# Group means of the normalisation in two PSUM banks, and a fold of the softmax sums moved behind a semaphore word, in a two-layer attention kernel

## The chip, the cores and the metric

The kernel runs on one core of one Trainium2 chip. The metric is the device time of one execution in microseconds (us), as the median over several executions. Five engines matter: TensorE (PE in the profile; PEld is its loading of weights), VectorE (DVE), ScalarE (ACT), GpSimd (POOL) and SyncE (SP, here only a queue that issues DMAs). GpSimd also issues DMAs, namely those that add to their target.

## The reference

The input x has 16 images of 256 channels by 32 by 32 positions, fp32. Two layers follow each other; each normalises in 16 groups along the last axis, runs attention with 4 heads of 64 channels over 1024 positions with a position term, and adds the result to x.

```python
def _gn(v, G=16, eps=1e-5):
    g = v.reshape(B_, H_, W_, G, C_ // G)
    m = jnp.mean(g, axis=(1, 2, 4), keepdims=True)
    s = jnp.var(g, axis=(1, 2, 4), keepdims=True)
    return ((g - m) / jnp.sqrt(s + eps)).reshape(v.shape)

q, k, v = proj(Wq, bq), proj(Wk, bk), proj(Wv, bv)      # 1x1 convolutions
sim  = jnp.einsum('bhdi,bhdj->bhij', q, k)
qpos = jnp.einsum('hdi,bhdj->bhij', (rel_h + rel_w).reshape(heads, d, n), q)
attn = jax.nn.softmax(sim + qpos, axis=-1)
x    = x + jnp.einsum('bhdn,bhmn->bhdm', v, attn)       # twice, for two layers
```

The part that the change touches is small arithmetic: the mean and the variance of each group, a sum over 128 partitions of a table of 16 columns, and the sums of the softmax.

## The kernel before

**Units and blocks.** A unit `u` is one image in one layer; there are 32, in the order of the list `units`. Each unit has four blocks `b` = 0 to 3: two pairs of heads (`pr`) times two halves of the query columns (`half` = `b` % 2). So there are 128 blocks, numbered `n`, and `block(n)` (from line 647) writes the instructions of all engines for one of them. The kernel schedules by hand: each engine executes its instructions in the order of this program text, and an instruction that waits holds up all that stand behind it on its engine.

**What a block does.** Eight score tiles `ps` of 128 by 1024 are made: VectorE first writes the position term into PSUM (`seed`, line 346), TensorE adds q k on top (`scores`, line 382), ScalarE takes the exponential into `p` (line 391), VectorE adds the `p` tiles up for the softmax sums (`add_up`, lines 400 and 402). Then TensorE forms v^T p in a PSUM tile `po` (`attend`, line 416). The seeds and first scores of the next block (`after`) are already made in the tail of the current one. Between them stand pieces of the next pair of heads or the next unit: projections q, k (line 265), values (line 295), position terms (line 323).

**Stretches and words.** All these products use TensorE as four tiles of 64 by 64, so that matmuls of the lower and the upper 64 rows run side by side. [...] So a product over 128 rows comes in two stretches: in the first the lower rows write bank 0 and the upper ones bank 1, in the second the other way round. Between the two stands a "word" (`stretches`, line 166): a one-element memset by GpSimd that waits for the last matmul of the first stretch, and for which the first matmul of the second stretch waits. In the text of a block, `values_of_p(0)` is the first stretch of v^T p, `values_of_p.word()` its word, `values_of_p(1)` its second stretch.

**The group means.** Unit `u + 2` is normalised while unit `u` is worked on. ScalarE sums the columns of each group (`norm_sums`, `norm_squares`, line 190). At the end of block 1 (`norm_mean`) and of block 3 (`norm_var`) TensorE sums over the partitions with a constant matrix `W.avg` (`mean_of_rows`, line 210) into `pm`, 16 columns of one bank, zeroed by VectorE (line 202). This too is a product in two stretches: `mean(0)` with the lower rows right after `values_of_p(0)`, then the scores of the next block's first tile, then `mean(1)` with the upper rows, then `values_of_p(1)`. `mean(1)` calls its own word on GpSimd. ScalarE takes the result out (`mean_out`): as the negated mean `neg` (line 220), or as `var` with epsilon added (line 232), after which GpSimd computes `rstd` by a power (line 234) and `nshift` (line 236). The next block, block 0 of the next unit, starts to apply them (`norm_apply`, line 245). Thirty units do this in the loop, that is 60 means.

**The softmax sums.** GpSimd's DMAs add, "fold", the accumulated tile of a block: the eighth `p` onto `acc` (`add_last`, line 433), the upper half of `acc` onto the lower (`fold`, line 438), parts onto a `stack` of the four sums of a pair of heads (SP in `stack_up`, line 452, and GpSimd in `fold_again`, line 457), and the stack onto itself with 64, 32, 16, 8 and 4 rows (`fold_stack`, line 462). Each fold of the stack needs the one before to have landed, and its issue on GpSimd waits for that. `spread_sums` (SP, line 470) distributes the result, `reciprocals` (lines 512 to 519) inverts it in the next block, and `finish` (lines 527 and 534) normalises the output and adds it to x.

**The order in the tail of a block with half = 1**, on GpSimd: the fold with 32 rows, `fold` of the previous block, the folds with 16 (`R // 2`) and 8 rows (`R // 4`), the word of v^T p, the word of the mean, the fold with 4 rows (`R // 8`), `fold_again`, in block 3 the power, and then, of the next block, `add_last` and the word `first.word()` of its first piece. On VectorE: the seed of the next block's first tile, the memset of `pm`, `add_up(5)`, the two instructions of `finish`, three seeds of the next block.

## Time and profile before

| | |
|---|---|
| runs | 2557.47 us median of 3 (2554.66 to 2560.26) |
| the profiled execution | 2574.55 us, span in the profile 2572.8 us |
| clock granted to TensorE | 0.997 of full speed, mean over the span |
| TensorE busy | 98% of the span |
| VectorE, ScalarE, GpSimd busy | 88%, 76%, 33% |
| matmuls of the means, line 210 | 30.3 us busy in all (15.3 and 15.0) |
| memsets of the words, line 166 | 190 |
| power on GpSimd, line 234 | 30, median 3.88 us each |

The profiled execution is 17 us longer than the median of the runs. Times of single instructions below are from the profiled execution. "Idle before" of a group is the time for which its engine stood still just ahead of it, and the profile names what ended that wait. A weight load (PEld) can wait without TensorE's stream standing still, since loads run ahead of matmuls.

### The profile page before, as it was taken

How to read it: one execution, taken by the hardware profiler on the slowest of the kernel's cores; microseconds unless marked ns; L12 is line 12 of the kernel's file. 1: busy time of each engine (PE TensorE's matmuls, PEld its weight loads, DVE VectorE, ACT ScalarE, POOL GpSimd, SP SyncE). 2: the span in 40 equal slices, each digit the busy share in tenths (PEclk: the TensorE clock that was granted, in tenths of full speed). 3: DMA queues.
4: the chain of work that ended last, by engine and by line, in shares of the span. 5: the costliest groups of instructions: out<-in, count | busy, mean ns of one | idle time of the engine just before them, and what ended most of it. 6: DMA issues, size and time to landing. Idle time of an engine off the chain costs nothing. (4 is left out here: it accounts for less than half of the span.)

```text
span 2572.8 us, 86074 instructions
## 1 busy us (share of the span) xinstructions
PE 2524.8 (98%) x37474; PEld 1739.3 (68%) x37474; DVE 2258.1 (88%) x2076; ACT 1956.9 (76%) x3934; POOL 837.4 (33%) x1254
## 2 busy tenths in 40 slices
PE   8999999999999999999999999999999999999997
PEld 4667776666777656666767777677776776666774
DVE  6888998888888889899888898898898998988997
ACT  6778777787777887777877777877778777787753
POOL 1232333323333233333233333333332333323320
PEclk9999999999999999999999999999999999999999
DMA  3344444444444444444444444444445444444441
GB/s 89 72 80 82 78 86 76 90 96 90 84 99 99 82 82 92 89 88 87 93 85 86 98 87 78 92 98 90 91 85 106 79 78 90 77 77 78 88 84 57
DMA packets 119539, 221.06 MB, mean 86 GB/s; under 512 B 53737, under 2 KB 55273, under 8 KB 119153
## 3 DMA queue, kind: packets, MB, share of 16 engines
q0 software_dynamic: 53568, 129.58, 30.3%
q1 hardware_dynamic: 65584, 85.90, 12.1%
q8 instruction: 295, 4.83, 0.8%
q14 instruction: 92, 0.75, 0.1%
HBM read 51.78 MB, written 17.30 MB: 27 GB/s over the span
## 5 line engine op out<-in xcount | busy, mean ns | idle before, releaser
L346 DVE TENSOR_TENSOR ps<-abt 128x1024 f32<-128x1024 f32 x1018 | 1225.7, 1227 | 279.3 <-ACT p L391 160.4
L391 ACT ACTIVATE p<-ps,shift 128x1024 f32<-128x1024 f32 x1024 | 1092.2, 1114 | 326.9 <-PE ps L382 237.5
L382 PE MATMUL ps<-q,k 64*64 64x512 f32 x8192 | 1016.3, 590 | 0.8 <-DVE ps L346 0.8
L416 PE MATMUL po<-p,v 64*64 64x256 f32 x16384 | 950.9, 378 | 0.0
L416 PEld LDWEIGHTS po<-p,v 64*64 64x64 f32 x16384 | 826.2, 133 | 140.9 <-issue 45.6
L402 DVE TENSOR_TENSOR acc<-acc,p 128x1024 f32<-128x1024 f32 x644 | 783.7, 1217 | 5.3 <-ACT p L391 0.5
L382 PEld LDWEIGHTS ps<-q,k 64*64 64x64 f32 x8192 | 409.5, 133 | 300.7 <-issue 186.7
L462 POOL DMA_DIRECT2D stack<-stack x310 | 254.1, 820 | 544.2 <-DMA stack<-stack 281.2
L166 POOL MEMSET token<- 1x1 f32 x380 | 47.9, 126 | 763.1 <-PE po L416 477.4
L295 PE MATMUL pv<-Wv,xn 64*64 64x256 f32 x4096 | 251.9, 376 | 2.4 <-POOL token L166 2.1
L265 PE MATMUL pq<-xn,Wq 64*64 64x512 f32 x2048 | 252.0, 593 | 0.3 <-DVE xn L906 0.3
L265 PE MATMUL pk<-xn,Wk 64*64 64x512 f32 x2048 | 250.4, 590 | 0.9 <-POOL token L166 0.9
L295 PEld LDWEIGHTS pv<-Wv,xn 64*64 64x64 f32 x4096 | 203.4, 133 | 56.7 <-issue 39.2
L457 POOL DMA_DIRECT2D stack<-acc x248 | 223.6, 1088 | 43.0 <-issue 29.7
L245 ACT ACTIVATE xn<-x,nshift,rstd 128x128 f32<-128x128 f32 x496 | 211.1, 500 | 16.3 <-POOL nshift L236 16.3
L190 ACT ACTIVATE junk<-x,neg 128x128 f32<-128x128 f32 x498 | 195.0, 400 | 0.0
L265 PEld LDWEIGHTS pq<-xn,Wq 64*64 64x64 f32 x2048 | 108.4, 134 | 112.3 <-issue 107.0
L438 POOL DMA_DIRECT2D acc<-acc x124 | 102.4, 826 | 251.6 <-DMA acc<-p 239.3
L477 ACT COPY od<-po 128x512 f32<-128x512 f32 x127 | 74.4, 586 | 129.1 <-PE po L416 129.1
L265 PEld LDWEIGHTS pk<-xn,Wk 64*64 64x64 f32 x2048 | 102.4, 134 | 100.3 <-issue 99.1
L433 POOL DMA_DIRECT2D acc<-p x124 | 131.3, 1059 | 98.8 <-DVE acc L402 80.1
L400 DVE TENSOR_TENSOR acc<-p,p 128x1024 f32<-128x1024 f32 x128 | 155.8, 1218 | 0.0
(75 smaller groups left out, 1238.3 us busy)
## 6 DMA issues: line engine op xcount, KB each, us to landing
acc<-p POOLq DMA_DIRECT2D x124, 512.0 KB, 5.2
rden<-rd SPq DMA_DIRECT2D x126, 256.0 KB, 4.1
acc<-acc POOLq DMA_DIRECT2D x124, 256.0 KB, 3.5
x<-in_x_dram SPq DMA_DIRECT2D x32, 512.0 KB, 4.3
stack<-acc SPq DMA_DIRECT2D x248, 64.0 KB, 2.1
stack<-acc POOLq DMA_DIRECT2D x248, 64.0 KB, 3.2
out_dram<-x SPq DMA_DIRECT2D x31, 512.0 KB, 4.3
stack<-stack POOLq DMA_DIRECT2D x62, 128.0 KB, 2.7
```

Of the source, the lines that this page charges most:

```text
L190: nc.scalar.activation(junk, grouped(xt[units[u][0]], g), func, accum_out=into[:, g : g + 1], **bias)
L245: nc.scalar.activation(grouped(xns[u], g), grouped(xt[units[u][0]], g), AF.Identity, bias=shift[:, g : g + 1], scale=rstd[:, g : g + 1],)
L265: yield nc.tensor.matmul(pk[c, nh, :], w[l][rs, cc, c0 : c0 + D], xns[u][rs, cc, nh * HALF : (nh + 1) * HALF], start=(t == 0 and cc == 0), ...
L295: yield nc.tensor.matmul(pv[c, a, i, :], xns[u][rs, cc, j0 : j0 + D], W.wv[l][rs, cc, :], start=(t == 0 and cc == 0 and i == 0), stop=(t = ...
L346: nc.vector.tensor_tensor(ps.rearrange("p h (w y) -> p h w y", y=H), ab[:, :, :H].unsqueeze(2).to_broadcast([P, 2, XH, H]), ab[:, :, H + h ...
L382: nc.tensor.matmul(ps[c, h, :], a[hs, j0 : j0 + D], b[hs, columns], start=bool(tag) and i == 0, stop=i == len(terms) - 1, skip_group_check ...
L391: nc.scalar.activation(p, ps, AF.Exp, bias=W.shift)
L400: nc.vector.tensor_tensor(accs[blk], probs[blk, 0], probs[blk, 1], ALU.add)
L402: nc.vector.tensor_tensor(accs[blk], accs[blk], probs[blk, j], ALU.add)
L416: yield nc.tensor.matmul(po[c, a, :QUART], vts[u][rs, j, c0 : c0 + D], p[rs, h, a * QUART : (a + 1) * QUART], start=(t == 0 and j == 0), s ...
L457: nc.gpsimd.dma_start(at, acc[R:D, h, :], accum_op=ALU.add)
L462: nc.gpsimd.dma_start(stack[:rows_], stack[rows_ : 2 * rows_], accum_op=ALU.add)
```

## The change

Four things change, in the functions of the means and in the text of `block`.

1. `mean_of_rows` sends the lower rows into bank 0 and the upper rows into bank 1 of `pm`, all four matmuls at once, ahead of the next block's first scores. There is no second stretch and no word. `filled` sets the columns in both banks (to 0 for the mean, to half of epsilon in each bank for the variance).
2. VectorE adds the two banks with a `tensor_reduce`, where ScalarE read one bank before. For the mean it negates. The constant `W.eps` and its memset go.
3. `mean_out` moves: it stood on ScalarE after the first scores; now it stands on VectorE behind `add_up(5)` and `finish`, ahead of the three seeds of the next block. On GpSimd, power and `nshift` are now written behind `finish` as before behind the folds.
4. The fold with 8 rows (`R // 4`) moves from ahead of `first(1)` to behind the word of v^T p. `fold_again` of the previous block comes next, and then the fold with 4 rows and `spread_sums`; before, these two stood ahead of `fold_again`. In blocks with half = 0, the seed of the next block's first tile is put ahead of `reciprocals`.

```diff
@@ -197,39 +197,42 @@
         for g in gs:
             of_group(u, g, AF.Identity, reds[u])
 
-    def zeroed(tag, name):
-        pm = psum2(tag, name)[:, 0, :G]
-        nc.vector.memset(pm, 0.0)
+    def filled(tag, name, value):
+        pm = psum2(tag, name)[:, :, :G]
+        nc.vector.memset(pm, value)
         return pm
 
     def mean_of_rows(pm, red):
 
-
-        def products(t):
-            for c in QUARTERS:
-                yield nc.tensor.matmul(
-                    pm[c, :], W.avg[QUARTERS[t], :D], red[QUARTERS[t], :],
+        for c in QUARTERS:
+            for a, rs in enumerate(QUARTERS):
+                nc.tensor.matmul(
+                    pm[c, a, :], W.avg[rs, :D], red[rs, :],
                     start=False, stop=True, skip_group_check=True,
                 )
 
-        return stretches(products)
-
     def norm_mean(u, pm):
+        mean_of_rows(pm, reds.pop(u))
+
         def out_of_psum():
             negs[u] = small.tile([P, G], F32, tag="neg", name=f"neg_{u}")
-            nc.scalar.mul(negs[u], pm, -1.0)
+            nc.vector.tensor_reduce(
+                negs[u], pm.rearrange("p a g -> p g a"), AX.X, ALU.add, negate=True
+            )
             sums[u] = small.tile([P, G], F32, tag="sum", name=f"sum_{u}")
 
-        return mean_of_rows(pm, reds.pop(u)), out_of_psum
+        return out_of_psum
 
     def norm_squares(u, gs):
         for g in gs:
             of_group(u, g, AF.Square, sums[u], bias=negs[u][:, g : g + 1])
 
     def norm_var(u, pm):
+        mean_of_rows(pm, sums.pop(u))
+
         def out_of_psum():
             var = small.tile([P, G], F32, tag="var", name=f"var_{u}")
-            nc.scalar.activation(var, pm, AF.Identity, bias=W.eps)
+            nc.vector.tensor_reduce(var, pm.rearrange("p a g -> p g a"), AX.X, ALU.add)
             rstd = small.tile([P, G], F32, tag="rstd", name=f"rstd_{u}")
             nc.gpsimd.tensor_tensor(rstd, var, W.mhalf[:, :G], ALU.pow)
             shift = small.tile([P, G], F32, tag="nshift", name=f"nshift_{u}")
@@ -237,7 +240,7 @@
             rss[u] = (rstd, shift)
             xns[u] = gnpool.tile([P, CC, N], F32, tag="gn", name=f"xn_{u}")
 
-        return mean_of_rows(pm, sums.pop(u)), out_of_psum
+        return out_of_psum
 
     def norm_apply(u, gs):
         rstd, shift = rss[u]
@@ -670,7 +673,6 @@
             fold(previous)
         if stacked:
             fold_stack(*stacked, R // 2)
-            fold_stack(*stacked, R // 4)
         first(1)
         first_out()
         seed(blk, 5, f0)
@@ -689,11 +691,11 @@
         scores(blk, 7)
         add_up(blk, 3)
         add_up(blk, 4)
+
+        if after:
+            seed(after, 0, f0)
         if summed:
             reciprocals(*summed)
-
-        if after:
-            seed(after, 0, f0)
         if n in check:
             next(checks)
         if b == 0 and one:
@@ -710,25 +712,27 @@
         values_of_p = attend(blk, po)
         values_of_p(0)
         if two and half == 1:
-            mean, mean_out = (norm_mean if b == 1 else norm_var)(u + 2, zeroed(f1, f"pm_{n}"))
-            mean(0)
+            if b == 1:
+                mean_out = norm_mean(u + 2, filled(f1, f"pm_{n}", 0.0))
+            else:
+                mean_out = norm_var(u + 2, filled(f1, f"pm_{n}", EPS / 2))
         if after:
             scores(after, 0)
         values_of_p.word()
-        if two and half == 1:
-            mean(1)
+        if stacked:
+            fold_stack(*stacked, R // 4)
+        if previous and folded:
+            fold_again(previous)
         if stacked:
             fold_stack(*stacked, R // 8)
             spread_sums(*stacked)
-        if previous and folded:
-            fold_again(previous)
         if half == 1 and u + 3 < NU and units[u + 3][1] == 0 and u > 0 or n == 3:
             load_x(units[u + 3][0], range(pr_, pr_ + 1) if u > 0 else range(CC))
-        if two and half == 1:
-            mean_out()
         add_up(blk, 5)
         if before:
             finish(*before)
+        if two and half == 1:
+            mean_out()
         if after:
             for j in range(1, 4):
                 seed(after, j, ring[j % 3])
@@ -1127,13 +1131,12 @@
         self.ident = new("ident", [P, P])
         make_identity(nc, self.ident)
         self.avg, self.ones = new("avg", [P, P]), new("ones", [P, P])
-        self.mhalf, self.shift, self.eps = new("mhalf", [P, sh.H]), new("shift", [P, 1]), new("eps", [P, 1])
+        self.mhalf, self.shift = new("mhalf", [P, sh.H]), new("shift", [P, 1])
         for t, v in (
             (self.avg, 1.0 / sh.COUNT),
             (self.ones, 1.0),
             (self.mhalf, -0.5),
             (self.shift, -SHIFT),
-            (self.eps, EPS),
         ):
             nc.vector.memset(t, v)
         both = range(len(layers))
```

## Prediction

> **What bounds the kernel now.** I read the shares of busy time first, then TensorE's waits, then the timeline of one disturbed and one undisturbed block. From the page:

> ```profile
> PE 2524.8 (98%) x37474; PEld 1739.3 (68%) x37474; DVE 2258.1 (88%) x2076; ACT 1956.9 (76%) x3934; POOL 837.4 (33%) x1254
> ```

> TensorE sets the time. A gain can only come from the 2% in which it stands still, or from fewer matmuls, and their number doesn't change. The waits of TensorE, as engine, line, what ended them, sum, times and longest in us:

> ```profile
> PE pm L210 <- POOL token L166: 20.0, 16, 2.8
> PE pv L295 <- POOL token L166: 2.1, 2, 1.1
> ```

> The one large entry is the second stretch of a mean, waiting for its word. GpSimd around a disturbed block, and TensorE beside it:

> ```profile
> 614.66 0.81 POOL L438 DMA_DIRECT2D acc<-acc  x1 [3.34 <-DMA acc<-p]
> 615.19 1.09 POOL L462 DMA_DIRECT2D stack<-stack  x1
> 620.56 0.81 POOL L462 DMA_DIRECT2D stack<-stack  x1 [4.29 <-DMA stack<-stack]
> 621.07 0.47 POOL L166 MEMSET token<- 1x1 f32 x2
> ```

> ```profile
> 617.68 1.10 PE L382 MATMUL ps<-q,k 64*64 64x512 f32 x7
> 621.60 0.23 PE L210 MATMUL pm<-red,avg 64*64 64x16 f32 x2 [2.82 <-POOL token L166]
> ```

> The fold at 620.56 (8 rows) could be issued only when the fold at 615.19 (16 rows) had landed, and both words stand behind it. The first stretch was over at 617.6, so GpSimd was late, not TensorE. It costs twice, as the windows of this stretch show (the first number after the engines is the granted clock):

> ```profile
> 617.00:621.60 4.60, 1.78 (x29) 0.76 (x21) 3.07 (x3) 2.07 (x5) 0.93 (x3) 1.00 0.29 58
> 621.60:625.20 3.60, 3.60 (x50) 3.60 (x54) 3.05 (x3) 2.12 (x6) 2.08 (x3) 0.69 0.07 7
> ```

> After the gap TensorE's clock is at half for 3.41 us. An undisturbed block 3, GpSimd with the power, then VectorE and ScalarE:

> ```profile
> 741.74 0.24 POOL L166 MEMSET token<- 1x1 f32 x2 [1.85 <-PE po L416]
> 742.27 0.80 POOL L462 DMA_DIRECT2D stack<-stack  x1 [0.30 <-issue]
> ...
> 744.16 3.73 POOL L234 TENSOR_TENSOR rstd<-var,mhalf 128x16 f32<-128x16 f32 x1
> ...
> 748.82 0.93 POOL L433 DMA_DIRECT2D acc<-p  x1 [0.22 <-issue]
> 750.41 0.09 POOL L166 MEMSET token<- 1x1 f32 x1 [0.66 <-PE pv L295]
> ```

> ```profile
> 742.57 1.28 DVE L534 SCALAR_TENSOR_TENSOR x<-od,bv,x 128x1024 f32<-128x1024 f32 x1
> 743.87 2.39 DVE L346 TENSOR_TENSOR ps<-abt 128x1024 f32<-128x1024 f32 x2
> ```

> ```profile
> 743.57 0.26 ACT L232 ACTIVATE var<-pm,eps 128x16 f32<-128x16 f32 x1
> ```

> To be seen: behind the power stands the next block's first word (750.41), here waiting for TensorE, so with room; and VectorE's seeds start at 743.87, just after ScalarE has read `pm` (743.83).

> **How much is lost.** From the list of matmuls I took, block by block, the gap between the last score matmul and the first one of the second mean stretch. It is 0.36 to 0.45 us in 42 of 60 blocks, and 0.55 to 3.41 in 18. The excess of those 18 over 0.41 sums to 23.2 us. The half-clock stretches after the two longest gaps (at 617 and 2353) cost 3.41 / 2 each, together 3.4 us. So 26.6 us of 2572.8 hang on late words. Two more stalls, at 829 and 1927, of 1.2 and 1.3 us, have another cause: there the power started over 3 us later than in the block shown, because GpSimd waited for other transfers, and the next block's first word was late.

> [...]

> **The change part by part.**

> *The word of v^T p goes ahead of the 8-row fold; the mean's word and second stretch go.* What is now ahead of the word on GpSimd is `fold` and the 16-row fold. In all 57 blocks that I looked at, that fold was issued at the latest 1.6 us before the end of the first stretch, so the remaining word is free in time, and comes 0.5 us after that end as in undisturbed blocks. All 18 gaps go: minus 23.2 us; and the two half-clock stretches: minus 3.4. What is late next is nothing on GpSimd before `values_of_p(1)`: in half = 0 blocks, with one word and no mean, the two stretches of v^T p lie 1.00 us apart (0.95 to 1.05) and TensorE shows no wait there.

> *The mean's matmuls.* Four as before, now in one piece. Undisturbed, the distance of the two stretches is 1.08 to 1.17 with a mean and 1.00 without, so a mean costs about 0.1 us; two changes of tile fewer, two row halves more at once. I take no difference; 0.05 either way is 3 us over 60.

> *The reduce on VectorE.* It stands ahead of three seeds that TensorE needs at once, on an engine that in these blocks works without a break from its fourth seed on. [...] the trace's nearest row, the 16-column read of `pm` (line 874), has 175 ns, and the next instruction started 92 ns after it did. So 0.09 to 0.19 us. Today a seed starts 1.23 us after the residual (line 534) in block 1, and 1.30 to 1.34 in block 3, since there it waits for ScalarE's read of `pm`; that wait goes. New start: 1.23 + 0.09 to 0.19 = 1.32 to 1.42. The third seed ends 0.20 us (median) before its first matmul in block 1 and from 0.055 in block 3, and 0.055 is the shortest distance in the trace. So the slack is 0.14 and about 0.02. Loss: 0 to 0.05 in block 1, 0 to 0.1 in block 3; I take 0.035, or 2 us over 60 blocks. The larger memset (72 ns, it moved the next instruction by 0.02) is inside this. The ScalarE read that goes (0.18 or 0.27 us) is hidden: ScalarE waits for TensorE there.

> *The later fold and GpSimd up to the next word.* Counted from the end of the first stretch, now: word 0.5, 8-row fold 0.65, two `fold_again` 1.2 and 1.9, then the 4-row fold, which waits for the 8-row one to land. From one issue to the next that took 2.6 to 3.9 us in the trace (once 5.6). So it goes at 3.3 to 4.5, and the power at 3.9 to 5.1, where it was 2.8 to 5.5 apart from the two late cases at 7.4 and 7.5. Its input `var` is ready at about 2.8 in either order. Power, `nshift`, `add_last` then lead to the next word: a power at 3.9 to 4.2 had the word at 9.2 (TensorE's own limit), one at 4.5 to 5.1 at 10.3 to 10.6, without a stall; the two late words at 12.5 lost 1.3, which puts the limit near 11.2, or a power at about 5.2. So most of the 30 blocks keep their cover; one or two landings over 3.9 us and 0.6 more in the two late cases cost about 2 us. `spread_sums` comes 1 to 2 us later; its reader is `reciprocals`, over 10 us away. ScalarE's `norm_apply` may start 1 us later, as it did after four powers without a stall. In block 1 no power follows and nothing is near.

> *The seed ahead of `reciprocals`, `W.eps`.* Nothing: in half = 0 blocks the seeds end 2 to 3 us early.

> *The sum.* Minus 26.6, plus 2 (reduce), plus 2 (GpSimd): minus 22.6 us, from 2574.55 to about 2552 in a profiled execution. The timed runs are 17.1 us shorter. If that is outside these stalls, they gain 22.6 too: 2535. If all of it is stall that they don't have (the spread of 5.6 us between runs is of this kind), 22.6 - 17.1 = 5.5 remains: 2552. An undisturbed block repeats to 0.02 us, which speaks for the first[...]. I take three quarters of the gain, 17: 2540.5.

> **The rivals.**

> *The timed runs have few late words.* Mechanism right, gain 5 to 8: 2550. For it, 17 us between profile and runs; against it, slack and late landings don't look like a product of the profiler.

> *VectorE becomes the bound in the tails.* If the reduce delays the seeds by 0.35 us, less a slack of 0.08 on average, that is 60 x 0.27 = 16 us back, and 2555 or so is left, about as before. For it, seeds end 0.06 us ahead of need in block 3; against it, the 92 ns after the nearest row.

> *Slower: GpSimd's tail makes the next block's first word late.* Place: block 3 into block 0, behind the power. Two DMAs' issue and a landing are now between the word and the power. It decides from the point where the power starts at 5.2 us; beyond it each us is lost 30 times. For a net loss over 5 us, 30 x d must exceed 17 + 5, so d over 0.73 us on average, a power at 5.9 and a landing of 4.7 in the usual block. At d = 0.9 it gives 2557.5 - 17 + 27 - 2 = 2565, more if gaps halve the clock. For it, one landing of 5.6; against it, 2.6 to 2.8 in most.

> *The word doesn't become free*, since `fold` ahead of it waits for a transfer too. The latest issue seen, 1.6 us ahead of need, speaks against it; it would leave part of the 23 us, and it is inside the second case.

> **How the numbers follow.** Forecast 0.60, few late words in the runs 0.19, VectorE as bound 0.11, GpSimd's tail 0.10. The forecast's own range is 2531 (all 22.6 and the matmuls' 3) to 2550; to leave out 2 in 10 the upper end goes to 2554, which takes in the rival with few late words. About 0.2%, 5 us, is what a measurement of this kernel can tell from no change; 2552.4 is that limit. Faster: all of the forecast, most of the second case and a part of the third, 0.80. Same: 0.10. Slower: 0.10.

> **What would show it.** In the changed kernel's profile: the wait of line 210 for the token gone, no half-clock stretch in the middle, the stretches of v^T p about 1.1 us apart in all blocks; the reduce under 0.2 us and line 382 not waiting for line 346; the power at 4 to 5 us after the first stretch and line 295 waiting for the token some 5 us in all. I am wrong if line 382 waits for seeds in most half = 1 blocks, or lines 295 and 265 for the token.

## The result, and the profile after

Over 14 runs each, the changed kernel takes 2554.88 us (2550.99 to 2562.13) and the kernel before 2560.22 us (2554.66 to 2571.41). The ratio is 0.9982, 95% interval 0.997 to 0.9995: a gain of about 5 us. The interval tells it from no change, but it is just under the 0.2% that the prediction took as its limit. The forecast was 2540.5 us, with a range of 2531 to 2554.

The profiled execution of the changed kernel is 2554.61 us long, its span 2552.8. That is nearly what the sum gave for a profiled execution, 2552. The sum started from a profiled execution of the kernel before of 2574.55 us, and none of the 14 runs was that slow. The near hit is luck in part: the changed kernel has new stalls of 9.6 us, where the sum had 2 us at another place, and older stalls and the two ends of the profile came out some 6 us shorter, which it did not contain at all.

The waits of TensorE in the changed kernel (line 268 is the projections' line 265 of before; engine, line, what ended the wait, sum in us, times, longest):

```profile
PE pk L268 <- POOL token L166: 7.0, 4, 2.7
PE pm L850 <- DVE first_red L840: 6.9, 3, 5.8
PE pm L876 <- DVE sum L871: 2.9, 1, 2.9
```

No mean waits for a word any more. A new wait stands first: the projection of k, second stretch, which is the first piece of block 1. The prediction had named this as a sign of being wrong ("or lines 295 and 265 for the token"): line 268 is its line 265.

An undisturbed block 3 on VectorE, to be compared with the residual at 742.57 and the seeds at 743.87 of before:

```profile
737.72 1.28 DVE L537 SCALAR_TENSOR_TENSOR x<-od,bv,x 128x1024 f32<-128x1024 f32 x1
738.92 0.18 DVE L235 TENSOR_REDUCE var<-pm 128x16 f32<-128x32 f32 x1
739.14 3.57 DVE L349 TENSOR_TENSOR ps<-abt 128x1024 f32<-128x1024 f32 x3
```

The seeds start 1.42 us after the residual, where it was 1.30. And GpSimd in the same block, to be compared with 741.74 to 750.41 of before:

```profile
736.88 0.09 POOL L166 MEMSET token<- 1x1 f32 x1 [3.18 <-PE pm L209]
737.35 0.81 POOL L465 DMA_DIRECT2D stack<-stack  x1 [0.38 <-issue]
...
740.86 0.81 POOL L465 DMA_DIRECT2D stack<-stack  x1 [0.97 <-DMA stack<-stack]
741.41 4.08 POOL L237 TENSOR_TENSOR rstd<-var,mhalf 128x16 f32<-128x16 f32 x1
...
746.15 0.94 POOL L436 DMA_DIRECT2D acc<-p  x1
746.81 0.32 POOL L166 MEMSET token<- 1x1 f32 x1
```

The word comes first, then the 8-row fold, and the power 4.5 us after the word (2.4 before). The next block's first word follows in time.

For the account I took from the list of matmuls the length of every block (from the start of v^T p to the next one) and its median by `b`. The median is that of an undisturbed block; what is more than 0.15 us above it, I call a stall.

| undisturbed span from the v^T p of this block to the next | before | after |
|---|---|---|
| b = 0 and 2 | 18.14, 18.16 us | 18.14, 18.16 us |
| b = 1 | 20.757 us | 20.828 us |
| b = 3 | 20.819 us | 20.871 us |
| sum of all stalls in blocks 0 to 125, first profile | 32.0 us | 10.8 us |
| the same, second profile (below) | 17.3 us | 11.0 us |

So the stalls of the profile of before went, the usual block with half = 1 became 0.05 to 0.07 us longer, and new stalls came. Three questions follow: was the profile of before a fair sample, what does the reduce cost, and where do the new stalls come from?

### The profile page after: what moved, and what is told of

Same layout as the page of the kernel before. It is cut to its first block, busy times and chain, and to the rows that moved or that the text cites. A ratio compares the mean times of both kernels' runs of the same rounds, so it can differ in the third digit from the quotient of the medians.

```text
span 2552.8 us, 86089 instructions
## 1 busy us (share of the span) xinstructions
PE 2520.5 (99%) x37474; PEld 1330.9 (52%) x37474; DVE 2263.9 (89%) x2135; ACT 1950.1 (76%) x3874; POOL 836.6 (33%) x1194
## 4 chain that ended last, share of the span: by engine, by line
PE 88%; DMA 3%; DVE 2%; POOL 1%; issue 1%; SPq 0%; ACT 0%; POOLq 0%; DVEq 0%; ACTq 0%
PE po L419 31%; PE ps L385 31%; PE pk L268 8%; PE pv L298 8%; PE pq L268 8%; PE pa L326 2%; DMA acc<-p 1%; DMA stack<-acc 1%; DVE acc L405 1%; DVE ps L349 1%; POOL rstd L237 1%; DMA acc<-acc 0%; POOL stack L460 0%; POOL stack L465 0%; POOL acc L436 0%
## 5 line engine op out<-in xcount | busy, mean ns | idle before, releaser
L385 PE MATMUL ps<-q,k 64*64 64x512 f32 x8192 | 990.2, 591 | 0.9 <-DVE ps L349 0.9
L419 PE MATMUL po<-p,v 64*64 64x256 f32 x16384 | 930.5, 376 | 0.0
L419 PEld LDWEIGHTS po<-p,v 64*64 64x64 f32 x16384 | 628.7, 133 | 364.7 <-issue 77.7
L385 PEld LDWEIGHTS ps<-q,k 64*64 64x64 f32 x8192 | 303.3, 133 | 406.5 <-issue 222.8
L465 POOL DMA_DIRECT2D stack<-stack x310 | 266.7, 860 | 372.8 <-DMA stack<-acc 155.3
L166 POOL MEMSET token<- 1x1 f32 x320 | 44.8, 140 | 853.9 <-PE po L419 426.9
L298 PE MATMUL pv<-Wv,xn 64*64 64x256 f32 x4096 | 244.3, 376 | 0.7 <-POOL token L166 0.4
L268 PE MATMUL pq<-xn,Wq 64*64 64x512 f32 x2048 | 244.3, 592 | 0.3 <-DVE xn L910 0.3
L248 ACT ACTIVATE xn<-x,nshift,rstd 128x128 f32<-128x128 f32 x496 | 211.1, 500 | 13.7 <-POOL nshift L239 13.7
L298 PEld LDWEIGHTS pv<-Wv,xn 64*64 64x64 f32 x4096 | 153.4, 133 | 102.8 <-issue 44.2
L268 PEld LDWEIGHTS pq<-xn,Wq 64*64 64x64 f32 x2048 | 78.6, 134 | 142.1 <-issue 129.9
L190 ACT ACTIVATE junk<-x 128x128 f32<-128x128 f32 x480 | 145.6, 314 | 0.0
```

The lines of the kernel that those rows point to most:

```text
L190: nc.scalar.activation(junk, grouped(xt[units[u][0]], g), func, accum_out=into[:, g : g + 1], **bias)
L248: nc.scalar.activation(grouped(xns[u], g), grouped(xt[units[u][0]], g), AF.Identity, bias=shift[:, g : g + 1], scale=rstd[:, g : g + 1],)
L268: yield nc.tensor.matmul(pk[c, nh, :], w[l][rs, cc, c0 : c0 + D], xns[u][rs, cc, nh * HALF : (nh + 1) * HALF], start=(t == 0 and cc == 0), ...
L298: yield nc.tensor.matmul(pv[c, a, i, :], xns[u][rs, cc, j0 : j0 + D], W.wv[l][rs, cc, :], start=(t == 0 and cc == 0 and i == 0), stop=(t = ...
L385: nc.tensor.matmul(ps[c, h, :], a[hs, j0 : j0 + D], b[hs, columns], start=bool(tag) and i == 0, stop=i == len(terms) - 1, skip_group_check ...
L419: yield nc.tensor.matmul(po[c, a, :QUART], vts[u][rs, j, c0 : c0 + D], p[rs, h, a * QUART : (a + 1) * QUART], start=(t == 0 and j == 0), s ...
```

## Experiments

### Second profiles of both kernels

No edit: both kernels again.

> The kernel before, unchanged, for a second profile. Theory (the profile that I forecast from was a slow draw): a span of 2553 to 2566 us, and the waits of the second mean stretch for the token 6 to 14 us instead of 20.0. Rival (the stalls are the same in every execution and something else makes the runs shorter): span shorter than 2572.8, waits for the token again 18 to 22 us.

Measured: span 2555.6 us.

```profile
PE pm L210 <- POOL token L166: 10.2, 10, 1.8
```

The wait is half as long. By the reckoning of the prediction (excess of the gap ahead of the second mean stretch over 0.41 us) it is 12.7 us in 14 blocks, not 23.2 in 18, and the clock never fell in the loop. So the rival is out; late words differ from execution to execution, and the first profile was a slow draw.

> The changed kernel, unchanged, for a second profile. Theory (word of the mean gone for good, new stalls at the first piece of block 1): no wait of line 210, the undisturbed half = 1 blocks again 0.05 to 0.07 us longer than before, line 268 or 298 waiting for the token 4 to 12 us. Rival (the 7.0 us of line 268 were chance): under 3 us.

Measured: span 2553.2 us, undisturbed blocks 20.827 and 20.871 us, no wait of a mean's matmuls (now line 209).

```profile
PE pk L268 <- POOL token L166: 6.8, 4, 2.2
```

The new wait is there again, 4 times, and in the same blocks: the spans of blocks 4, 28, 40 and 84, each up to the v^T p of a block 1, are too long in both profiles, by 9.6 and 9.4 us together. This is more than the waits, since TensorE's clock also fell to half once, in block 4, in both (in the first for 3.41 us, from 140.6 us on). The stall belongs to the kernel, not to chance.

### The parts alone

The fold's move alone, with the means as before:

```diff
             fold_stack(*stacked, R // 2)
-            fold_stack(*stacked, R // 4)
...
         values_of_p.word()
         if two and half == 1:
             mean(1)
         if stacked:
-            fold_stack(*stacked, R // 8)
-            spread_sums(*stacked)
+            fold_stack(*stacked, R // 4)
         if previous and folded:
             fold_again(previous)
+        if stacked:
+            fold_stack(*stacked, R // 8)
+            spread_sums(*stacked)
```

The seed ahead of `reciprocals` is in it too.

> Fold with 8 rows behind the word, fold_again ahead of the fold with 4 rows, seed ahead of reciprocals; the means as before in two stretches with ScalarE. Theory: it is the fold ahead of the words that made them late, so all late words of the means go here too, and the blocks keep their old length: 2548 to 2553 us, ratio 0.996 to 0.998, better than the whole change by about 3 us. Rival (the second stretch and its word are what is late): waits of line 210 stay over 8 us, ratio 0.998 to 1.001.

Measured: 2556.34 us over 11 runs beside 2561.02, ratio 0.9979 (0.9968 to 0.999). Its profile has no wait of line 210 at all, though the mean still has its second stretch and its own word; blocks 1 and 3 have their old lengths, 20.757 and 20.819. And the new stall is there without the new means:

```profile
PE pk L265 <- POOL token L166: 6.2, 3, 2.6
```

The profile agrees with the theory: the fold made the words late. The seed's move shows no effect: blocks 0 and 2 keep their 18.14 and 18.16 us. The ratio agrees too, while the 3 us over the whole change don't show: the two intervals overlap, and the new stalls, over 4 us in each of two blocks of this profile, use it up.

The means alone, with folds and reciprocals where they were (the edit is the rest of the change's diff):

> The means in two banks with VectorE's reduce behind finish; folds and reciprocals where they were. Theory: the word of v^T p still stands behind the fold with 8 rows, so the late words stay and only their place changes (line 419 waits for the token instead of 210), and the reduce adds 3 to 4 us: ratio 1.000 to 1.003. Rival (the mean's second stretch costs the time): 0.996 to 0.998.

Measured: 2558.86 us over 22 runs, ratio 0.9992 (0.9984 to 1.0). In its profile another instruction waits for the late word:

```profile
PE po L419 <- POOL token L166: 9.9, 8, 2.0
```

Line 419 is v^T p. The second stretch and its word of the mean were never the cause; they only stood where the wait showed. The ratio is just below what was expected, next to no difference. Blocks 1 and 3 are 20.828 and 20.865 us long: the cost of the means is in this half of the change. Where the 3.5 us or so that these blocks cost were won back was not tried.

### The price of the reduce

ScalarE reads the first bank alone, at its old place; the sums over the upper 64 rows are left out:

```diff
-            nc.vector.tensor_reduce(
-                negs[u], pm.rearrange("p a g -> p g a"), AX.X, ALU.add, negate=True
-            )
+            nc.scalar.mul(negs[u], pm[:, 0, :], -1.0)
```

and likewise for `var`, with a constant matrix of twice the weight.

> The changed kernel without VectorE's reduce: ScalarE reads the first bank alone, at its place of before. The sums over the upper 64 rows are left out of mean and variance, the lower ones are weighted double; all four matmuls stay. Theory (the reduce delays the seeds): undisturbed blocks 1 and 3 are back at 20.76 and 20.80 to 20.82 us. Rival (the four matmuls in one piece make them longer): 20.83 and 20.87 us stay.

Measured: undisturbed blocks 1 and 3 at 20.757 and 20.817 us, as before. So it is the reduce and its place, not the four matmuls in one piece, nor the larger memset of `pm`, which this kernel keeps. (Its span of 2555.3 us holds 8.4 us of waits of the projection of k, more than the 7.0 of the changed kernel.)

The same reduce twice in a row, the second one into a spare tile:

```diff
             nc.vector.tensor_reduce(var, pm.rearrange("p a g -> p g a"), AX.X, ALU.add)
+            twin = small.tile([P, G], F32, tag="twin", name=f"twin_{u}_v")
+            nc.vector.tensor_reduce(twin, pm.rearrange("p a g -> p g a"), AX.X, ALU.add)
```

> The changed kernel with each reduce issued twice. Theory: the seeds come 0.22 us later and nothing is left to cover it, so undisturbed blocks 1 and 3 become 20.83 + 0.2 and 20.87 + 0.2 us, 12 to 13 us in all: a span of 2563 to 2568 us. Rival (VectorE has cover): under 0.05 us more per block, 2553 to 2556 us.

Measured: span 2558.9 us, blocks 1 and 3 at 20.925 and 20.969 us, 0.097 us more each. That is half of what was expected, and more than the rival had. VectorE's timeline shows why:

```profile
741.09 0.18 DVE L239 TENSOR_REDUCE var<-pm 128x16 f32<-128x32 f32 x1
741.19 0.18 DVE L241 TENSOR_REDUCE twin_v<-pm 128x16 f32<-128x32 f32 x1
741.41 3.53 DVE L355 TENSOR_TENSOR ps<-abt 128x1024 f32<-128x1024 f32 x3
```

A reduce behind a reduce starts 0.10 us later; the seed starts 0.22 us after the reduce, that is after its end (0.184). The seed writes over `pm`. Whether it starts late for that reason wasn't tried. What the doubling adds is the 0.10, and TensorE pays all of it, so behind the first reduce nothing covers VectorE in these tails.

### The load of x

Where do the new stalls begin? GpSimd in the changed kernel, from block 27 (a block 3) to block 29 (a block 1):

```profile
586.93 0.94 POOL L436 DMA_DIRECT2D acc<-p  x1
587.61 0.30 POOL L166 MEMSET token<- 1x1 f32 x1
590.23 0.09 POOL L166 MEMSET token<- 1x1 f32 x1 [2.33 <-PE pq L268]
596.52 0.84 POOL L441 DMA_DIRECT2D acc<-acc  x1 [6.20 <-DMA acc<-p]
600.01 0.09 POOL L166 MEMSET token<- 1x1 f32 x1 [2.64 <-PE po L419]
603.84 1.69 POOL L460 DMA_DIRECT2D stack<-acc  x2 [3.74 <-DMA stack<-acc]
609.89 0.84 POOL L465 DMA_DIRECT2D stack<-stack  x1 [4.37 <-DMA stack<-acc]
610.43 1.23 POOL L436 DMA_DIRECT2D acc<-p  x1
611.01 0.69 POOL L166 MEMSET token<- 1x1 f32 x1
```

and SP beside it:

```profile
584.75 2.42 SPq L473 DMA_DIRECT2D den_all<-stack  x4
587.21 0.58 SPq L107 DMA_DIRECT2D x<-in_x_dram  x1
587.89 0.38 SPq L539 DMA_DIRECT2D out_dram<-x  x1
```

The same two DMAs of GpSimd in the first profile of before, from the same block:

```profile
588.20 0.91 POOL L433 DMA_DIRECT2D acc<-p  x1
595.39 0.84 POOL L438 DMA_DIRECT2D acc<-acc  x1 [4.95 <-DMA acc<-p]
```

Read from the end: the first word of block 1 (611.01) stands behind the 64-row fold (609.89), which waits for `fold_again` (603.84), which waits for `stack_up`, which waits for `fold` (596.52), which waits 6.20 us for `add_last` (586.93). And just beside `add_last`, of 512 KB, SP issues the load of the next image, of 512 KB: it stands behind `spread_sums` in SP's queue, and `spread_sums` waits for the 4-row fold, which the change has put later. From `add_last` to `fold` it is 9.59 us here, and 7.19 in the lines of before.

Of the 30 later blocks 3, 12 load an image half, so the other 18 can be set against them. On average over these 12, the load came 8.0 us after the first stretch of v^T p before, and 9.4 us after the change.

| behind block 3, averages | load against `add_last` | `add_last` to `fold`, 12 with a load | 18 without |
|---|---|---|---|
| before, two profiles | 1.7 us ahead, both | 6.13, 6.12 us | 5.30, 5.25 us |
| after, two profiles | 0.1 us behind, both | 7.28, 7.34 us | 5.68, 5.73 us |
| fold's move alone | 0.3 us behind | 7.60 us | 5.43 us |
| load ahead (next run) | 10.5 us ahead | 5.62 us | 5.62 us |

Blocks without a load are 0.1 to 0.5 us slower with the fold moved, in the last row too; the rest depends on the load's place. Behind block 1 it went the other way: there the load moved from 0.5 or 0.8 us ahead of `add_last` to 2.2 or 2.5 us behind it, and the distance with a load fell from 6.8 and 6.6 to 6.1 and 6.0 us. So what counts is that the two are issued close together. The stalls of blocks 4, 28, 40 and 84 all follow a block 3 with a load.

The first of these stalls, in block 4, has another part. The block ahead of it (number 3) loads two halves of an image, and did so beside `add_last` before the change too:

```profile
114.09 0.93 POOL L433 DMA_DIRECT2D acc<-p  x1 [0.21 <-issue]
124.18 0.82 POOL L438 DMA_DIRECT2D acc<-acc  x1 [5.82 <-DMA acc<-p]
```

and after:

```profile
115.18 0.94 POOL L436 DMA_DIRECT2D acc<-p  x1
125.17 0.83 POOL L441 DMA_DIRECT2D acc<-acc  x1 [7.34 <-DMA acc<-p]
```

The distance is 10.1 us before and 10.0 after. But `add_last` itself comes 12.5 us after the start of this block's v^T p, where it came 10.9 us after it: it stands behind the power, which starts at 8.0 us instead of 6.2. This one stall is 4.6 of the 9.6 us (4.2 of 9.4 in the second profile). That the later power is a cause of it is read from these times; it was not tried alone.

So in the changed kernel I put the load ahead of the folds in the text, hence ahead of `spread_sums` on SP:

```diff
         values_of_p.word()
+        if half == 1 and u + 3 < NU and units[u + 3][1] == 0 and u > 0 or n == 3:
+            load_x(units[u + 3][0], range(pr_, pr_ + 1) if u > 0 else range(CC))
         if stacked:
             fold_stack(*stacked, R // 4)
...
-        if half == 1 and u + 3 < NU and units[u + 3][1] == 0 and u > 0 or n == 3:
-            load_x(units[u + 3][0], range(pr_, pr_ + 1) if u > 0 else range(CC))
```

> The changed kernel with the load of the next image put ahead of the 8-row fold in the text, so ahead of spread_sums in SP's queue. Theory (the fold's later place pushes the load of x from 7.5 to 10 us after the first stretch, into the 512 KB transfer of add_last, and that makes the first word of block 1 late): the distance from add_last to fold in block 0 falls from 6.3 to 5.7 us, the waits of line 268 for the token from 7 to under 2 us, 2549 to 2552 us by the runs' median, ratio 0.996 to 0.997. Rival (the load is not what delays add_last): line 268 still waits 5 to 8 us, ratio 0.998.

Measured: 2545.98 us over 5 runs (2545.24 to 2549.22) beside 2563.93, ratio 0.994 (0.9926 to 0.9953), more than was expected. The distance from `add_last` to `fold` no longer depends on a load (last row of the table). The waits for the token are nearly gone:

```profile
PE pv L298 <- POOL token L166: 0.8, 4, 0.2
```

The same stretch, from block 27 on:

```profile
582.55 0.94 POOL L436 DMA_DIRECT2D acc<-p  x1
...
589.10 0.84 POOL L441 DMA_DIRECT2D acc<-acc  x1 [4.31 <-DMA acc<-p]
594.47 0.09 POOL L166 MEMSET token<- 1x1 f32 x1 [4.53 <-PE po L419]
595.18 1.69 POOL L460 DMA_DIRECT2D stack<-acc  x2 [0.62 <-DMA stack<-acc]
600.52 0.84 POOL L465 DMA_DIRECT2D stack<-stack  x1 [3.64 <-DMA stack<-acc]
601.05 1.23 POOL L436 DMA_DIRECT2D acc<-p  x1
602.78 0.09 POOL L166 MEMSET token<- 1x1 f32 x1 [0.49 <-PE pk L268]
```

`fold` follows 6.55 us after `add_last`, 3.0 us sooner than in the changed kernel; by the 64-row fold the chain is 5.0 us sooner, and now the word (602.78) waits for TensorE. That the load's place decides is shown, for the stall of block 4 too, which goes although `add_last` is late there in this run as well (13.7 us after the start of v^T p). The store to `out_dram`, too, is issued close to `add_last` in both kernels (587.89 beside 586.93, and 582.79 beside 582.55 with the load ahead), so it is not what delays it. By what means a load so close delays `add_last` was not shown.

The load ahead, with the fold's move and the means as before:

> The run with the fold's move alone (means as before in two stretches), with the load of x ahead of the folds in the same way. Theory: neither late words nor the reduce: 2546 to 2550 us, ratio 0.995 to 0.9965. Rival: as the run with the fold's move alone, 0.998.

Measured: 2544.53 us over 5 runs (2544.02 to 2546.6), ratio 0.9932 (0.9918 to 0.9945); the undisturbed blocks at 20.757 and 20.819 us. This too is more than was expected. It is the fastest version of the study, by its median, and beats both kernels. Over the run before, with the new means, it is 1.45 us by the medians, with overlapping ranges; the undisturbed blocks say 3.6.

And the kernel before with nothing but the load put ahead of the 4-row fold:

> The kernel before with nothing but the load of x put ahead of the 4-row fold and of spread_sums. Theory (in the kernel before, the late words come from the fold with 8 rows ahead of them; its load at 7.5 us is not yet in the way of add_last): the waits of line 210 stay at 6 us or more, ratio 0.997 to 1.000. Rival (the early load is what gives the gain, with or without the fold's move): ratio 0.993 to 0.995, waits of line 210 under 3 us.

Measured: 2554.57 us over 10 runs beside 2560.55, ratio 0.9977 (0.9964 to 0.9989), and

```profile
PE pm L210 <- POOL token L166: 8.8, 13, 1.7
```

The late words of the means stay, so the load isn't what makes them. Its early place is worth something by itself, and each of the two moves alone gives about 0.2%; together they give 0.7%, more than their sum. Each move leaves, or makes, a stall that the other one takes away.

## Why the prediction was wrong

Two steps failed: a term of the sum that was read off one slow profile, and the statement that the later fold costs nothing beyond its own reader. A third term, the reduce, was too low.

**Right: the mechanism of the late words.** They came from the 8-row fold ahead of the words, all waits of line 210 for the token are gone in both profiles after the change, and the half-clock stretches at these places with them (a new one came in block 4).

**Wrong in size: "minus 23.2 us; and the two half-clock stretches: minus 3.4".** This term was read off one profile. A second one of the same kernel had 12.7 us and no half-clock stretch in the loop. The prediction weighed this ("the timed runs have few late words", 5 to 8 us, chance 0.19) and then took three quarters of the gain. The measured gain is as large as this rival's, about 5 us, but only in part for its reason, so its number is partly luck: 12.7 us of late words, less the 4 us that the prediction put against them, would have left about 9. The new stalls and the reduce took the rest. The run with the load ahead, set against the run with the load alone, gives 0.994 to 0.9977, again about 9 us. The argument that an undisturbed block repeats to 0.02 us was true and beside the point, since what differs between runs is the number of disturbed ones.

**Wrong: the step on the later fold.** "`spread_sums` comes 1 to 2 us later; its reader is `reciprocals`, over 10 us away." The first half is right (from 5.0 to 6.5 us after the first stretch in block 3). But `spread_sums` isn't alone on SP: the load of x stands behind it, was pushed from 8.0 to 9.4 us in block 3, and that made the chain behind `add_last` late. A stall was looked for behind the power, from block 3 into block 0, at about 2 us in all. There the power started at 4.1 to 6.2 us, forecast at 3.9 to 5.1, and stalls behind block 3 came to 0.8 us in the first profile: the cover held. (The power's places of before were read too narrowly: beside 2.8 to 5.5 us and the two late cases, two blocks with late words had it at 5.9 and 6.3.) The stall came one block later, from block 0 into block 1: 7.0 us of waits in one profile and 6.8 in the other, with blocks 9.6 and 9.4 us longer. The prediction followed the reader of the moved instruction, and not what stands behind it in its queue; and it followed the later power to the next block's first word, and not on through `add_last` to the block after it.

**Too low: the reduce.** Taken at 0.09 to 0.19 us, which was an estimate, and 2 us in all; it lasted 0.184 us. The seed starts 0.22 us after the reduce and 1.42 us after the residual, the upper end of the forecast. Blocks 1 and 3 are 0.071 and 0.052 us longer, and 30 of each make 3.7 us. The seeds of an undisturbed block start about 0.19 and 0.11 us later than before, so the slack was about 0.12 us in block 1 and 0.06 in block 3, judged at 0.14 and 0.02. The nearest row (line 874 of before, 0.175 us, with 92 ns to the next start) was followed by an instruction that didn't touch the tile just read.

**Right: the matmuls of the mean.** In one piece or two, no difference shows: without the reduce the blocks have their old length. No kernel here is written so that the two row halves write one bank at a time. Whether a product over 128 rows needs its two stretches and the word between them was therefore not shown.

The balance, from the second profile of before to the first one after: stalls minus 6.5 (17.3 to 10.8, of which 12.7 of late means went and others came), longer blocks plus 3.7, together minus 2.8. Measured between the two spans: 2555.6 to 2552.8, minus 2.8 too. That the two are equal is partly luck: up to the first v^T p the second of these profiles is 1.1 us longer, and from there to the last one it is 3.8 us shorter. Between the medians of the runs it is minus 5.3, and from the profile that was forecast from it would be minus 20.

## What to carry to other kernels

When an instruction moves, follow the queue of every DMA that depends on it, not only its own reader: a load that merely stands behind it moves too, and may be issued close to another large transfer (here 7.3 us from `add_last` to `fold`, and 5.6 with the load well ahead). A wait at an engine names the last link; here the second stretch of the mean showed the wait, and removing that stretch alone only handed the wait to the next reader of the same queue. Where stalls vary between executions, one profile isn't a sum to take off: compare its length with all timed runs first, and if it is longer than all of them, forecast from the stall that a run of median length can hold.
